# An RWKV block with AdaLN and an FP4 FFN: the last FFNs by chunks in two streams, small weights in one array, FP4 in place

## The chip, the cores and the metric

The kernel runs on one core of a Trainium2 chip. The time is the device time of one execution in microseconds (us). Before the change it is 3216.84 us, the median of three runs (3215.44 to 3220.56). Engine names are those of the profile: PE is the matrix engine (PEld its weight loads), DVE the vector engine, ACT the scalar engine, POOL is GpSimd, SP the engine that issues the DMAs (SPq its queue).

## The reference

The input x is 2 batches of 4096 tokens of 256 channels. Six rows per batch (sa, ca, ga, sb, cb, gb) come from a conditioning vector c: mod = (silu(c) @ wmod).

```python
h = _layernorm(x) * (1 + ca) + sa
x = x + ga * rwkv(h)              # two layers, then a layer norm
h = _layernorm(x) * (1 + cb) + sb
x = x + gb * ffn(h)

# each rwkv layer:
x = x + time_mix(ln(x))           # mixes with the token before, r, k, v, g, decay w, a linear
                                  # recurrence over 4096 tokens, 4 heads of 64
x = x + channel_mix(ln(x))        # sigmoid(. @ cWr) * (relu(. @ cWk)**2 @ cWv), 256 -> 768 -> 256

def ffn(x):                       # 256 -> 704 -> 256
    gate, y = fp4_linear(x, w_gate), fp4_linear(x, w_up)
    return fp4_linear(silu(gate) * y, w_down)
```

fp4_linear rounds both of its operands in blocks of 16 along the last dimension: the block is divided by its largest magnitude over 6, rounded to the grid 0, 0.5, 1, 1.5, 2, 3, 4, 6, and multiplied back. So each FFN rounds its input (256 columns), its hidden row (704 columns) and, once, its weights.

## The kernel before, in words

All arithmetic is in float32. A batch is cut into 16 tiles of 256 tokens (TT), two chunks of 128 (C = 2) each, 32 tiles in all. A tile passes through first_layer, second_layer and ffns, each a Python generator; there are two streams of the first layer (one per batch), two of the second, one for all FFNs, one for the FFN weights and one for the conditioning rows.

The instructions are not issued as the generators yield them. A Plan (lines 104 to 318) records each operation with its costs and its dependences (record, need), and run (from line 280) takes from up to 24 recorded operations of each stream the one that it thinks can start first, by its own table of durations. A stream only records more while the stock of free tiles has at least its number of the tuple LEAST (8, 5, 3). All instructions are given out by line 262, so nearly every row of the profile has that line, and the names of the tiles tell them apart. What the planner chooses is fixed when the program is built: on the chip each engine takes its queue in that order and waits on semaphores.

Tiles: 36 slots of 514 columns, 4 double slots, 24 tiny tiles for row statistics, 5 long tiles of 768 columns for the FFN, 5 PSUM banks (bank), pa and kv for the recurrence.

- The loads (lines 484 to 558): cT in two DMAs, per layer 14 vectors of 256 numbers (vec), w1 in four pieces, w2a, w2b in two, five matrices, td1 and td2 in four pieces, cWk, cWv, cWr, and the modulation weights. The vectors are spread over the partitions number by number. All are issued by SP.
- fp4 (lines 566 to 601): seven DVE operations and one on ACT: largest magnitude, scale, reciprocal, a product into y, the step bits into p, two additions of a large multiple of the step, ACT's subtraction of MAGIC, a product into the destination. It uses the source, y and p; all calls share one tile scales.
- conditioning (from line 1107): the row of ln_out_w lies in one partition of the slot lnw, and POOL's partition_broadcast (line 1118) copies it to all 128 in another slot.
- ffn_weights (from line 1147): after ten steps of the first layer it loads w_gate, w_up and w_down by 128 rows, rounds them, and transposes them on PE.
- ffns (from line 1245), one stream: per tile, layer norm, FP4 of both chunks at once (512 columns), transposes; then, chunk after chunk, gate and up (wg, wu: four groups of 352 columns), FP4 of 704 columns, six transposes, the down product wd, and a multiplication by gb into half of the slot ob. After both chunks POOL adds x over 512 columns and SP stores the tile.

Nothing in ffns records chunk 1 before chunk 0's operations are recorded, and a tile begins after the one before.

Of the kernel before, what the change touches and what calls it, by code (L numbers as in the profile page):

```python
# [37 lines left out]
TINY = 24  # L38
# [3 lines left out]
FFN_SHARE = 1.4  # L42
# [3 lines left out]
MAGIC = 1.5 * 2.0**22  # L46

# [7 lines left out]
    "L0_ffn_w_up", "L0_ffn_w_down", "L0_c", "L0_wmod",  # L55
]
# [47 lines left out]
class Plan:  # L104
# [174 lines left out]

    def run(self, streams, stock):  # L280
        streams = [Stream(*q) for q in streams]
        while True:
# [24 lines left out]
            if not can:  # L307
                assert all(st.gen is None and not st.queue for st in streams), "stuck"
                return
# [72 lines left out]
def rwkv_adaln_fp4_kernel(ctx: ExitStack, tc: tile.TileContext, a: dict, out: bass.AP):  # L382
# [74 lines left out]
    scales = wk.tile([P, 3 * (FI // QB)], F32, name="scales")  # L457

    def take_slot():
        return pl.take(stock)  # L460
# [4 lines left out]
    def give(*ts):  # L465
        stock.extend(ts)
# [23 lines left out]
    with nc.allow_non_contiguous_dma(reason="two vectors of 256"):  # L490
        for b in range(B):
            load(cT[:, :, b], a["L0_c"][b].rearrange("(k p) -> p k", p=P))
# [12 lines left out]
    load(lnw[:1, :D], a["L0_attn_ln_out_w"].unsqueeze(0))  # L505

    def load_mat(name, src, kc):
# [5 lines left out]
    VECS = ["ln1_w", "ln2_w", "x_maa", "w_maa", "k_maa", "v_maa", "r_maa", "g_maa",  # L513
            "gn_w", "gn_b", "ck_maa", "cr_maa", "time_decay", "time_first"]
    lay = []
    for i in range(L):
        w = {}
        vec = const.tile([P, len(VECS), J], F32, name=f"vec{i}")
        for n, v in enumerate(VECS):
            src = a["L0_attn_" + v][i]  # L520
            if v.startswith("time"):
                src = src.rearrange("h k -> (h k)")
            with nc.allow_non_contiguous_dma(reason="a vector of 256"):
                load(vec[:, n, :], src.rearrange("(j p) -> p j", p=P))
            w[v] = vec[:, n, :]

        w1 = a["L0_attn_tm_w1"][i].rearrange("(k p) n -> p k n", p=P)
        w["w1"] = wp.tile([P, J, 8 * E], F32, name=f"w1_{i}")  # L530
        load(w["w1"][:, :, : 5 * E], w1)
        for m in range(5, 8):
            load(w["w1"][:, :, m * E : (m + 1) * E], w1[:, :, 4 * E :])
        w2 = a["L0_attn_tm_w2"][i].rearrange("f e d -> (f e) d")
        w2a = wp.tile([P, D], F32, name=f"w2a_{i}")
        load(w2a, w2[0:P, :])
        w2b = wp.tile([2 * E, D], F32, name=f"w2b_{i}")
        for m in range(2):
            load(w2b[m * E : (m + 1) * E, :], w2[P : 5 * E, :])
        w["w2"] = [w2a[E * f : E * (f + 1), :] for f in range(4)]  # L540
        w["w2b"] = w2b
        for n in ("Wr", "Wk", "Wv", "Wg", "Wo"):
            w[n] = load_mat(f"{n}_{i}", a["L0_attn_" + n][i], J)
        w["wvm"] = const.tile([P, J * H], F32, name=f"wvm{i}")
        w["centred"] = False
        w["td1"] = wp.tile([P, J, 2 * ED], F32, name=f"td1_{i}")
        w["td2"] = wp.tile([2 * ED, D], F32, name=f"td2_{i}")
        for m in range(2):
            load(
                w["td1"][:, :, m * ED : (m + 1) * ED],  # L550
                a["L0_attn_td_w1"][i].rearrange("(k p) n -> p k n", p=P),
            )
            load(w["td2"][m * ED : (m + 1) * ED, :], a["L0_attn_td_w2"][i])
        w["cWk"] = load_mat(f"cWk_{i}", a["L0_attn_cWk"][i], J)
        w["cWv"] = load_mat(f"cWv_{i}", a["L0_attn_cWv"][i], FD // P)
        w["cWr"] = load_mat(f"cWr_{i}", a["L0_attn_cWr"][i], J)
        lay.append(w)
        load_wmod(1 + i)
# [7 lines left out]
    def fp4(nc, src, n, rows, dst, st, y, p):  # L566
# [10 lines left out]

        def blk(t):
            return t[:rows, :n].rearrange("p (b q) -> p b q", q=QB)

        am, sc, inv = (st[:rows, m * (FI // QB) : m * (FI // QB) + nb] for m in range(3))
        sb = src.rearrange("p (b q) -> p b q", q=QB)
        nc.vector.tensor_reduce(am, sb, AX.X, ALU.max, apply_absolute_value=True)
# [4 lines left out]
        nc.vector.scalar_tensor_tensor(blk(y), sb, DOWN, invb, ALU.mult, ALU.mult)  # L588
        nc.vector.tensor_scalar(
            p[:rows, :n].bitcast(I32), y[:rows, :n].bitcast(I32), STEP_BITS, None, ALU.bitwise_and  # L590
        )
        yield
        yv, pv = y[:rows, :n], p[:rows, :n]
        nc.vector.scalar_tensor_tensor(yv, pv, MAGIC, yv, ALU.mult, ALU.add)
        nc.vector.scalar_tensor_tensor(yv, pv, -MAGIC, yv, ALU.mult, ALU.add)
        nc.scalar.activation(yv, yv, AF.Copy, bias=MAGIC)
        yield
        nc.vector.scalar_tensor_tensor(
            dst.rearrange("p (b q) -> p b q", q=QB), blk(y), MAGIC, scb, ALU.subtract, ALU.mult
        )  # L600
# [506 lines left out]
    def conditioning():  # L1107
# [5 lines left out]
        lnb_s, wide_s, tmp_s = take_slot(), take_slot(), take_slot()  # L1113
        lnb = lnb_s[:, :D]
# [3 lines left out]
        pl.gpsimd.partition_broadcast(lnb, lnw[:1, :D])  # L1118
# [25 lines left out]
        give(lnb_s, wide_s, tmp_s, lnw)  # L1144
        tiny.append(few)

    def ffn_weights():
# [3 lines left out]
        for src, dst in ((a["L0_ffn_w_gate"], wg), (a["L0_ffn_w_up"], wu)):  # L1151
            for n0 in range(0, FI, P):
                n = min(P, FI - n0)
                wt, y, p = (pl.take(long) for _ in range(3))
                pl.sync.dma_start(out=wt[:n, :D], in_=src[n0 : n0 + n, :])
                yield from fp4(pl, wt[:n, :D], D, n, wt[:n, :D], scales, y, p)
# [9 lines left out]
                long.extend((wt, y, p))  # L1166
                yield
        for m in range(J):
            wt, y, p = (pl.take(long) for _ in range(3))
            pl.sync.dma_start(out=wt[:, :FI], in_=a["L0_ffn_w_down"][m * P : (m + 1) * P, :])  # L1170
            yield from fp4(pl, wt[:, :FI], FI, P, wt[:, :FI], scales, y, p)
# [10 lines left out]
            long.extend((wt, y, p))  # L1182
# [62 lines left out]
    def ffns():  # L1245
        HF = FI // 2
        while "ffn" not in known:
            yield
        for _ in range(B * NT):
            while not done:  # L1250
                yield
# [5 lines left out]
            xf = xn.rearrange("p c d -> p (c d)")  # L1257
            y_s, p_s = pl.take(long), pl.take(long)
            yield from fp4(pl, xf, C * D, P, xf, scales, y_s, p_s)
            long.extend((y_s, p_s))  # L1260
# [5 lines left out]
            give(xn_s)  # L1266
            yield
            ob_s = take_slot()
            ob = v3(ob_s)
            for c in range(C):  # L1270
                cs_ = slice(c * P, (c + 1) * P)
                hb_s = pl.take(long)
                hb = hb_s[:, :FI]
                for s in range(2):
                    fs = slice(s * HF, (s + 1) * HF)
                    bk, gp = pl.bank()
                    for k in range(J):
                        mm(gp[:, :HF], xqT[:, k, cs_], wg[:, k, fs], k == 0, k == J - 1)
                    pl.scalar.activation(hb[:, fs], gp[:, :HF], AF.Sigmoid)
                    pl.vector.tensor_tensor(hb[:, fs], hb[:, fs], gp[:, :HF], ALU.mult)  # L1280
                    pl.close(bk)
                    yield
                    bk, up = pl.bank()
                    for k in range(J):
                        mm(up[:, :HF], xqT[:, k, cs_], wu[:, k, fs], k == 0, k == J - 1)
                    pl.vector.tensor_tensor(hb[:, fs], hb[:, fs], up[:, :HF], ALU.mult)
                    pl.close(bk)
                    yield
                y_s, p_s = pl.take(long), pl.take(long)
                yield from fp4(pl, hb, FI, P, hb, scales, y_s, p_s)  # L1290
                long.extend((y_s, p_s))
                hT_s = pl.take(long)
                hT = hT_s.rearrange("p (f n) -> p f n", f=NF)
                for g in range(2):
                    bk, pt = pl.bank()
                    for f in range(3):
                        at0 = f_at[3 * g + f]
                        tr(pt[:, f * P : (f + 1) * P], hb[:, at0 : at0 + P])
                    pl.scalar.copy(
                        hT[:, 3 * g : 3 * g + 3, :], pt[:, : 3 * P].rearrange("p (f n) -> p f n", f=3)  # L1300
                    )
                    pl.close(bk)
                    yield
                long.append(hb_s)
                bk, y = pl.bank()
                for f in range(NF):
                    mm(y[:, :D], hT[:, f, :], wd[:, f, :], f == 0, f == NF - 1)
                pl.vector.tensor_tensor(ob[:, c, :], y[:, :D], rows["gb"][b], ALU.mult)
                pl.close(bk)
                long.append(hT_s)  # L1310
                yield
            give(xq_s)
            pl.gpsimd.tensor_tensor(ob, ob, x1, ALU.add)
            pl.sync.dma_start(out=rows_of(out, b, t), in_=ob)
            give(ob_s, x1_s)
            yield

# [4 lines left out]
    with tc.manual_schedule():  # L1322
        streams += [(ffns(), LATE[2], LEAST[2]), (ffn_weights(), 2.0, 0), (conditioning(), -1.0, 0)]
        pl.run(streams, stock)

# [20 lines left out]
```

## Time and profile before

| | |
|---|---|
| median of three runs | 3216.84 us |
| the profiled execution | 3216.25 us |
| its span, first to last instruction | 3214.5 us |
| mean granted PE clock | 0.970 |
| PE busy | 3034.9 us, 94% |
| DVE busy | 2386.1 us, 74% |
| ACT, POOL busy | 1621.0 us, 937.6 us |
| moved by DMA | 42.31 MB, 13 GB/s mean |

The profile divides the span into 40 slices and gives each engine a digit, its busy share in tenths. The table of stages gives busy microseconds of each engine in a chosen stretch, with the number of instructions in brackets, then the granted clock of PE (1.00 is full speed), the mean busy share of the 16 DMA engines and what they moved in GB/s. In the timeline a line begins with the start and the duration in us; in square brackets stands how long the engine had been idle, and who released it. A line of the waits gives the total in us, how often, and the longest. Transposes are matmuls with ident. A float32 matmul shows as two instructions.

### The profile page before, as it was taken

To read this page: it belongs to the slowest core of one execution; us is meant where nothing else is said; L and a number is where in the kernel's file an instruction comes from. 1 tells how busy PE (TensorE), PEld (TensorE's weight loads), DVE (VectorE), ACT (ScalarE), POOL (GpSimd) and SP (SyncE) were. 2 spreads that over 40 slices of the span, in tenths; PEclk is the share of its full clock that TensorE was granted. 3 is DMA by queue.
4 is the path that set the end of the run, shared out by engine and by line. 5 is a ranking of instruction groups with operands and counts; after the bars stand their busy time and mean duration, and the time that the engine had idled before them with its cause. 6 is when DMAs were issued, how large, how long until landed. Compare 5 with 4: busy or idle time off the path is not lost.

```text
span 3214.5 us, 88104 instructions
## 1 busy us (share of the span) xinstructions
PE 3034.9 (94%) x37948; PEld 2423.3 (75%) x37948; DVE 2386.1 (74%) x6146; ACT 1621.0 (50%) x3244; POOL 937.6 (29%) x857
## 2 busy tenths in 40 slices
PE   3899999999999999999999999999999999999875
PEld 2677778787777778788777777878787787778653
DVE  4687777787877777777777876787787787777764
ACT  1465554555555555555555454555554555554321
POOL 1233332232323333223223232233233233322210
PEclk7899999999999999999999999999999999999987
DMA  4000000000000000000000000000000000000000
GB/s 130 17 20 5 9 8 8 12 15 8 9 8 8 15 9 15 8 6 11 8 15 8 8 11 5 18 5 14 8 9 8 12 11 9 11 2 14 12 4 10
DMA packets 46856, 42.31 MB, mean 13 GB/s; under 512 B 13185, under 2 KB 44930, under 8 KB 46466
## 3 DMA queue, kind: packets, MB, share of 16 engines
q1 hardware_dynamic: 46466, 36.68, 3.8%
q8 instruction: 298, 4.88, 0.6%
q14 instruction: 92, 0.75, 0.1%
HBM read 28.28 MB, written 8.39 MB: 11 GB/s over the span
## 4 chain that ended last, share of the span: by engine, by line
PE 77%; DVE 10%; ACT 6%; issue 3%; POOL 1%; DMA 1%; SPq 1%; POOLq 0%; DVEq 0%; ACTq 0%
PE bank L262 69%; PE pa L262 7%; DVE slot L262 5%; ACT slot L262 3%; DVE long L262 2%; ACT attn L262 2%; DVE tiny L262 1%; PE kv L262 1%; DVE scales L262 1%; POOL slot L262 1%; SPq L485 1%; DVE diag L262 1%; ACT L262 1%; ACT long L262 1%; POOL tiny L262 0%
## 5 line engine op out<-in xcount | busy, mean ns | idle before, releaser
L262 POOL TENSOR_TENSOR slot<-slot,slot 128x512 f32<-128x512 f32 x416 | 503.5, 1224 | 980.0 <-DVE slot L262 692.5
L262 ACT ACTIVATE slot<-bank 128x512 f32<-128x512 f32 (+1 forms) x644 | 338.2, 530 | 692.7 <-PE bank L262 662.1
L262 POOL TENSOR_TENSOR tiny<-tiny,nhalf 128x2 f32<-128x2 f32 (+1 forms) x288 | 291.6, 1015 | 957.5 <-DVE tiny L262 867.3
L262 DVE TENSOR_TENSOR slot<-slot,slot 128x512 f32<-128x512 f32 x512 | 382.7, 749 | 102.4 <-PE pa L262 86.3
L262 PE MATMUL bank<-slot,cWk 128*128 128x256 f32 x1536 | 367.4, 385 | 2.8 <-DVE slot L262 1.7
L262 PE MATMUL bank<-cWv,slot 128*128 128x256 f32 x1536 | 344.1, 380 | 0.0
L262 PEld LDWEIGHTS pa<-slot 64*32 64x32 f32 x19456 | 222.1, 108 | 140.3 <-issue 54.6
L262 PEld LDWEIGHTS bank<-slot,cWk 128*128 128x128 f32 x1536 | 286.4, 191 | 45.7 <-DVE slot L262 2.8
L262 PEld LDWEIGHTS bank<-cWv,slot 128*128 128x128 f32 x1536 | 289.3, 190 | 39.6 <-ACT slot L262 0.3
L262 ACT ACTIVATE slot<-bank,vec 128x256 f32<-128x256 f32 x512 | 233.1, 496 | 154.2 <-PE bank L262 145.7
L262 DVE TENSOR_TENSOR slot<-slot,bank 128x512 f32<-128x512 f32 x192 | 131.0, 682 | 225.8 <-PE bank L262 203.6
L262 PE MATMUL pa<-slot 64*32 64x16 f32 x19456 | 264.2, 190 | 30.4 <-DVE slot L262 10.6
L262 DVE SCALAR_TENSOR_TENSOR slot<-bank,vec,slot 128x256 f32<-128x256 f32 x640 | 273.7, 473 | 18.8 <-PE bank L262 18.2
L262 POOL TENSOR_TENSOR slot<-slot 128x512 f32<-128x512 f32 x128 | 142.1, 1112 | 329.2 <-ACT slot L262 278.4
L262 DVE TENSOR_TENSOR long<-long,bank 128x352 f32<-128x352 f32 x256 | 131.8, 515 | 91.3 <-ACT long L262 67.6
L262 PE MATMUL bank<-ident,slot 128*128 128x128 f32 x1152 | 177.6, 282 | 23.1 <-ACT slot L262 15.9
L262 ACT ACTIVATE slot<-slot,tiny 128x256 f32<-128x256 f32 x256 | 142.1, 594 | 111.8 <-DVE tiny L262 90.3
L262 PE MATMUL bank<-wd,long 128*128 128x256 f32 x768 | 191.6, 402 | 0.2 <-ACT slot L262 0.2
L262 DVE SCALAR_TENSOR_TENSOR slot<-slot,vec,slot 128x256 f32<-128x256 f32 x384 | 179.3, 503 | 12.6 <-POOL slot L262 12.5
L262 ACT ACT_TABLE_LOAD x137 | 175.8, 1283 | 19.2 <-PE bank L262 9.5
L262 ACT COPY slot<-bank 128x512 f32<-128x512 f32 x224 | 130.0, 583 | 103.5 <-PE bank L262 99.5
L262 PE MATMUL bank<-wg,slot 128*128 128x352 f32 x512 | 177.8, 470 | 4.1 <-ACT slot L262 4.1
(112 smaller groups left out, 5796.3 us busy)
## 6 DMA issues: line engine op xcount, KB each, us to landing
slot<-in_L_attn_x_dram SPq DMA_DIRECT2D x64, 256.0 KB, 2.7
out_dram<-slot SPq DMA_DIRECT2D x32, 256.0 KB, 2.2
slot<-in_L_wmod_dram SPq DMA_DIRECT2D x6, 256.0 KB, 6.7
cWk<-in_L_attn_cWk_dram SPq DMA_DIRECT2D x2, 768.0 KB, 5.9
cWv<-in_L_attn_cWv_dram SPq DMA_DIRECT2D x2, 768.0 KB, 6.6
long<-in_L_ffn_w_down_dram SPq DMA_DIRECT2D x2, 352.0 KB, 2.8
long<-in_L_ffn_w_gate_dram SPq DMA_DIRECT2D x5, 128.0 KB, 4.9
long<-in_L_ffn_w_up_dram SPq DMA_DIRECT2D x5, 128.0 KB, 2.0
```

The source lines that it names most:

```text
L262: fn(*[real(v) for v in a], **{n: real(v) for n, v in k.items()})
L485: nc.sync.dma_start(out=dst, in_=src)
```

## The change

1. The loads. Two arrays are made from the inputs ahead of the launch: small, 1564 columns for each layer, which holds the 14 vectors, w1, td1, w2a, w2b and td2 in the form in which the kernel uses them, and cT. One DMA loads each layer's array. The names w["w1"] and so on become views of it.
2. The row ln_out_w is loaded into all 128 partitions by one DMA with a broadcast source; partition_broadcast is gone, and so is its slot.
3. fp4 works in the tile that holds its source (y is the source); it takes one further tile p. There are three tiles scales, one for inputs and weights, and one per chunk.
4. ffns becomes ffn_inputs, ffn_chunk and ffn_chunks. For all but the last three tiles ffn_inputs runs the chunks itself, one after the other. For the last three (FFN_TAIL) it puts them into the list ready[c], and two further streams, one per chunk number, take them from there; the next tile's input is begun when both lists are shorter than FFN_AHEAD.
5. Each chunk has its own output slot, an add on POOL of 256 columns and a store of 128 rows.
6. 16 tiny tiles in place of 24. When no recorded operation can start, a new function press lets one stream record more, whatever the stock.

```diff
-TINY = 24
+TINY = 16
+FFN_TAIL = 3
+FFN_AHEAD = 1
...
+    def press(self, streams):
+        for st in sorted(streams, key=lambda st: st.least):
...
             if not can:
+                if self.press(streams):
+                    continue
...
-    load(lnw[:1, :D], a["L0_attn_ln_out_w"].unsqueeze(0))
+    load(lnw[:, :D], a["L0_attn_ln_out_w"].unsqueeze(0).to_broadcast([P, D]))
...
-        vec = const.tile([P, len(VECS), J], F32, name=f"vec{i}")
+        small = wp.tile([P, SMALL], F32, name=f"small{i}")
+        load(small, a["small"][i])
...
-    def fp4(nc, src, n, rows, dst, st, y, p):
+    def fp4(nc, t, n, rows, st, p):
...
+        y, pv = t[:rows, :n], p[:rows, :n]
+        yb = y.rearrange("p (b q) -> p b q", q=QB)
...
+        nc.vector.scalar_tensor_tensor(yb, yb, DOWN, invb, ALU.mult, ALU.mult)
+        nc.vector.tensor_scalar(pv.bitcast(I32), y.bitcast(I32), STEP_BITS, None, ALU.bitwise_and)
+        yield
+        nc.vector.scalar_tensor_tensor(y, pv, MAGIC, y, ALU.mult, ALU.add)
+        nc.vector.scalar_tensor_tensor(y, pv, -MAGIC, y, ALU.mult, ALU.add)
+        nc.scalar.activation(y, y, AF.Copy, bias=MAGIC)
+        yield
+        nc.vector.scalar_tensor_tensor(yb, yb, MAGIC, scb, ALU.subtract, ALU.mult)
...
-        pl.gpsimd.partition_broadcast(lnb, lnw[:1, :D])
...
+    def ffn_inputs():
...
+        for n in range(B * NT):
+            while not done or max(len(q) for q in ready) >= FFN_AHEAD:
                 yield
...
+            for c in range(C):
+                if n < B * NT - FFN_TAIL:
+                    yield from ffn_chunk(c, b, t, x1_s, xq_s, left)
+                else:
+                    ready[c].append((b, t, x1_s, xq_s, left))
...
+    def ffn_chunks(c):
+        for _ in range(FFN_TAIL):
+            while not ready[c]:
                 yield
+            yield from ffn_chunk(c, *ready[c].pop(0))
...
+        pl.gpsimd.tensor_tensor(ob, ob, x1[:, c, :], ALU.add)
+        pl.sync.dma_start(out=rows_of(out, b, t)[:, c, :], in_=ob)
...
+        streams += [(ffn_inputs(), LATE[2], LEAST[2]), *((ffn_chunks(c), LATE[2], 1) for c in range(C)), (ffn_weights(), 2.0, 0), (conditioning(), -1.0, 0)]
```

ffn_chunk is the body of the loop over c of ffns, with scales[1 + c], a p tile of its own, and the slot ob_s taken at the scaling.

## The prediction

> **What bounds it now.** I read the page first: engine shares, then the 40 slices.
>
> ```profile
> PE 3034.9 (94%) x37948; PEld 2423.3 (75%) x37948; DVE 2386.1 (74%) x6146; ACT 1621.0 (50%) x3244; POOL 937.6 (29%) x857
> ...
> PE   3899999999999999999999999999999999999875
> ...
> PEclk7899999999999999999999999999999999999987
> ```
>
> PE is busy in 94% of the span, and the missing part lies in the first and the last slices. The table of stages gives it in us (columns: PE, weight loads, DVE, ACT, POOL, clock, DMA).
>
> ```profile
> 300.00:2950.00 2650.00, 2609.01 (x33224) 2095.83 (x33223) 2028.14 (x5218) 1416.52 (x2824) 816.72 (x728) 0.99 0.03 10
> ```
> ```profile
> 3147.00:3165.40 18.40, 9.97 (x34) 7.03 (x34) 10.72 (x23) 2.67 (x5) 0.87 (x1) 0.78 0.00 0
> 3165.40:3185.00 19.60, 11.65 (x38) 8.13 (x38) 11.80 (x21) 3.89 (x7) 1.26 (x1) 0.76 0.04 13
> ...
> sum 117.60, PE 63.11 PEld 44.15 DVE 63.13 ACT 17.53 POOL 6.40; mean PE 9.02 PEld 6.31 DVE 9.02 ACT 2.50 POOL 0.91
> ```
>
> In the middle PE idles 41 of 2650 us: it is the bound, and only less PE work would help there. In the last 117.6 us (from 3096.9, when the last channel mix leaves PE) PE and DVE are each busy 63 us, taking turns. The waits of PE after 2950 name the turn:
>
> ```profile
> PE bank L262 <- DVE long L262: 48.3, 6, 9.4
> ```
>
> Six times PE waits for one FP4 rounding on DVE, with nothing else to do: five times 7.3 to 8.5 us, once 9.4. The start, from the timeline (PE, POOL, SP, DVE):
>
> ```profile
> 14.36 6.62 PE L262 MATMUL bank<-slot,slot 128*128 128x512 f32 x8 [14.36 <-DMA slot<-in_L_wmod_dram]
> 36.51 1.39 PE L262 MATMUL bank<-ident,slot 128*128 128x128 f32 x4 [15.54 <-ACT slot L262]
> 56.34 0.69 PE L262 MATMUL bank<-ident,long 128*128 128x128 f32 x2 [18.43 <-DVE long L262]
> ```
> ```profile
> 25.23 0.55 POOL L262 PARTITION_BROADCAST slot<-slot  x1 [6.29 <-issue]
> 34.90 0.73 POOL L262 TENSOR_TENSOR tiny<-tiny,nhalf 128x2 f32<-128x2 f32 x1 [9.12 <-issue]
> ```
> ```profile
> 45.35 16.92 SPq L262 DMA_DIRECT2D long<-in_L_ffn_w_gate_dram  x4
> ```
> ```profile
> 52.61 0.42 DVE L262 TENSOR_REDUCE scales<-long 128x16 f32<-128x256 f32 x1 [16.79 <-DMA long<-in_L_ffn_w_gate_dram]
> ```
>
> PE stops at 21 and works steadily only from 56.34. The first stop is POOL's: around one partition_broadcast of 0.55 us it does nothing else from 18.94 to 34.90, and the layer norm's power stands behind it. The second is the first w_gate tile: its load is issued last, at 45.35, lands at 52.6, and DVE rounds it until 56.34 (3.73 us). PE takes its queue in order, so the first projection waits behind that tile's transposes.
>
> **Start: small weights in one array, row spread by its load.** Ahead of w_gate, SP now issues 77 loads of vectors, matrices, modulation weights and x, about 0.5 us each, until 45. In the order of the changed program it issues 28 loads ahead: 14 us by the same step. What remains is bytes: the layer arrays hold 0.80 MB each, the matrices and the rest bring it to 10.25 MB including the first w_gate tile, nearly what moves today. Between 16 and 26 us the DMA queue moved 309 GB/s at 97% busy, and its best slices 381; from 2.8 us (issue at 0.7, first landing 2.1 later) the tile lands at 29.7 (381) to 36.0 (309). I take 33, between the two, as many of the packets that slowed the 309 stretch (704 of 3077 under 512 B) are gone. With 3.73 of rounding PE resumes at 36.7 instead of 56.34: **minus 20** (16.6 to 23). The other chain, layer norm of the first x, has its power input at 23.2 today and needs 5.9 more (34.90 to the end of the lerp in today's steps), or 29 to 31; it is the next in line, so 26 is the most.
>
> Against it: layer 0's array and seven matrices now stand ahead of the modulation weights, 4.21 MB to their end: 13.9 to 16.4 us where PE starts at 14.36 today. That costs at most 2, before the w_gate wait, and is hidden by it. The broadcast's removal alone is worth nothing: PE would wait for w_gate. The row's own load grows from 1 to 128 KB, 0.4 us of the queue at 309 GB/s, counted in the bytes. The page "DMA: Bandwidth & Descriptors", section "Anatomy of one DMA", of the Trainium skill prices transfers at 2.0 us plus bytes at 436 GB/s; by that estimate the tile would land near 26 and the layer norm's chain would decide, 26 us saved in place of 20; no stretch here holds that rate.
>
> **Tail: the last three FFNs by chunks in two streams.** Row prices, DVE: FP4 of 704 columns 0.88+0.20+0.42+0.94+0.54+1.86+0.94=5.78, with ACT's 0.79 and gaps 6.65 (3178.38 to 3185.03); FP4 of 512: 4.46, with ACT 5.1; a gating product 0.52. PE: a gate or up group 1.18 (3191.59 to 3192.78), six transposes 1.5, twelve down matmuls 4.4 to 5.3 after a wait. I call T0 the end of the last channel mix on PE, and walk the changed order from there:
> - DVE does the channel mix's end and most of the last tile's two layer norms, 6 us, until tile 31's first gate is there at T0+8 (PE first has six and four transposes and one down product). Then in its order: 8 products (4.2), two FP4 (11.6), two scalings (0.8), and of the last tile the norm's rest (2.5) and FP4 (4.5): 23.6, to T0+31. The last tile's own input is ready at about T0+26.
> - PE: two groups of it, then transposes of tile 31's second chunk at T0+31 (1.5), a group (1.2), a down product (4.2), two groups (2.4): T0+40.5.
> - Last tile, chunk 0: its FP4 with chunk 1's products between is 10.3, to T0+51; transposes and down to 56.7; chunk 1's FP4 has ended at 55 beside that; transposes 1.5, down 4.4: 62.6; scaling 0.4, POOL add 1.0, store 3.05 (3211.45 to the end): **T0+67**, against 117.6 now.
> - T0 itself is later: five groups, six transposes and a down product now stand before it: 5.9+1.5+2.8 (the down product takes 2.76 at 1517 us, full clock) = 10. PE idled 12.5 in 2950 to 3096.9, which may hide part; I count none as hidden.
> Gain 117.6-67-10: **minus 40**. Low end 20: if each of the three tiles still exposes one FP4 (3x6.65). High end 50: if the 12.5 idle us take the moved work.
>
> The clock enters here: in the tail's rows it is 0.76 to 0.78, and 0.99 in the middle; the down product takes 4.74 at 3166.93 and 2.76 at full clock. The page "TensorE: Matmul & The Clock Gate", section "HAM oscillation", says that the clock halves after an idle gap over some 3.4 us; by that rule the 10 us gap before the last chunk would still make the end cold, so the end would not speed up; were the gaps shorter than that, four down products would save some 1.7 us each, 7 in all, by that estimate. My walk keeps the slow price after each wait.
>
> **Middle: FP4 in place, chunked adds and stores.** FP4 has the same seven DVE operations and one ACT; only the tile that holds the result changes, and a chunk holds two long tiles, not three. Both programs have the same 19,760 matmuls of the same shapes. One 128x512 POOL add (1.22) becomes two of 128x256, which the trace does not show: between 0.82 (128x2) and 1.22 each, so 0.4 to 1.2 more a tile, 13 to 39 over 32 tiles; POOL is 29% busy, and while POOL's other adds stand behind these, PE, 98% busy there, has other streams' work. 32 more stores at about 0.4 of SP's time hide in a DMA share of 0.03. Tables: 129 loads, not 137 (1.28 each), on ACT at 50%. Tiny tiles 24 to 16 and three scale tiles: no wait on them above 1.4 us now. The planner's order is new throughout, so PE's 41 us of waits may move either way: 0, with plus or minus 15 (a third of them).
>
> **Sum.** 3214.5-20-40 = 3154.5. The profiled execution took 3216.25, 1.75 more than its span, and lies 0.6 under the median of 3216.84: **3157**.
>
> **Rivals.**
> - One end only, **3177**: either the start keeps its wait (bytes at under 200 GB/s would do it, as the 124 GB/s of 26 to 37 us show can happen when SP issues slowly), or DVE, with 22.5 us a tile against PE's 21.6 (the two rows above, added), becomes the tail's bound and each tile exposes an FP4. For: DVE and PE are level in the tail. Against: one FP4 beside the other chunk's groups is what the changed order has on both engines.
> - No measurable change (within 0.2%, 6.4 us, about what this measurement can tell): the middle loses the 60.
> - Slower, **3253**: PE's order in the middle is fixed at build time, and a chunk's transposes stand in it where the planner thinks FP4 done. If they stand too early, PE waits in each of 29 tiles for three FP4s (input and two chunks). The waits of PE on DVE's long tiles between 300 and 2950 are three, 1.5 us in all, the longest 1.1: 87 x 1.1 = 96 on 3157. It decides from 0.76 us a wait. For: FFN work is placed anew. Against: the same rounding, the same planner, and 1.5 us of such waits now.
>
> **Numbers.** Forecast 0.68 (3133 to 3172: start 16.6 to 26, tail 31 to 50, middle as above), one end only 0.20 (3172 to 3195), no change 0.04, slower 0.08. Faster 0.88. The range 3130 to 3190 leaves out the last two and a part of the second.
>
> **What would show it.** Start: PE's first transposes of w_gate at 33 to 40 us, no gap on POOL before the second power, SP's w_gate issue near 15. Tail: PE's waits on long after the last channel mix from 48 to under 20 us, the span from there 67 and not 117.6, PE and DVE busy side by side. Middle: 41 us idle of 2650, give or take 15. I am wrong if PE resumes after 45, if the FFN streams wait for each other's tiles, or if PE's idle time between 300 and 2950 rises above 60.

## The result, and the profile after

The changed kernel takes **3185.45 us** (median of four runs, 3183.25 to 3188.18), the kernel before 3216.41 beside it (3215.44 to 3220.56): ratio 0.9902, 95% interval 0.9885 to 0.9919. That is 28 us over the predicted 3157 and inside the range of 3130 to 3190, but outside the forecast's own band of 3133 to 3172. The profiled execution took 3185.40 us, its span is 3183.6.

The page of the kernel after, engine shares and two rows of the slices:

```profile
PE 3034.4 (95%) x37948; PEld 2428.1 (76%) x37948; DVE 2390.7 (75%) x6146; ACT 1616.2 (51%) x3236; POOL 951.1 (30%) x888
...
PE   5899999999999999999999999998999999999987
...
PEclk8899999999999999999999999999999999999989
```

PE is busy for as long as before (3034.9), so the 31 us that the span lost are idle time of PE. The first digit went from 3 to 5, the last two from 7 and 5 to 8 and 7. Between them a single 8 is new, in the slice from 2149 to 2229 us; a wait of 7.3 us in it belongs to the hole that the experiments come back to. The start in the timeline of after (PE, then DVE, POOL, SP):

```profile
14.34 5.11 PE L271 MATMUL bank<-slot,slot 128*128 128x512 f32 x8 [14.34 <-DMA slot<-in_L_wmod_dram]
23.64 0.33 PE L271 MATMUL bank<-ident,slot 128*128 128x128 f32 x1 [4.19 <-ACT slot L271]
...
35.96 0.69 PE L271 MATMUL bank<-ident,long 128*128 128x128 f32 x2 [10.93 <-DVE long L271]
```
```profile
32.23 0.42 DVE L271 TENSOR_REDUCE scales<-long 128x16 f32<-128x256 f32 x1 [9.28 <-DMA long<-in_L_ffn_w_gate_dram]
```
```profile
22.05 0.70 POOL L271 TENSOR_TENSOR tiny<-tiny,nhalf 128x2 f32<-128x2 f32 x1 [4.33 <-DVE tiny L271]
```
```profile
24.72 14.55 SPq L271 DMA_DIRECT2D long<-in_L_ffn_w_gate_dram  x5
```

The first matmul stands where it stood; the w_gate tile lands at 32.2 and no longer at 52.6, and PE goes on at 35.96 and not at 56.34. POOL's power (of the layer norm) is at 22.05, not at 34.90. Stages of after (columns as before: PE, weight loads, DVE, ACT, POOL, clock, DMA):

```profile
300.00:2950.00 2650.00, 2582.99 (x33007) 2072.34 (x33006) 2004.55 (x5137) 1386.82 (x2770) 814.00 (x741) 0.99 0.03 10
...
3125.25:3145.00 19.75, 13.22 (x54) 9.13 (x52) 18.87 (x45) 4.51 (x9) 2.47 (x3) 0.97 0.02 7
3145.00:3165.00 20.00, 19.25 (x72) 14.41 (x72) 12.07 (x23) 5.05 (x10) 2.03 (x2) 0.86 0.04 13
3165.00:3183.60 18.60, 9.19 (x36) 7.20 (x36) 9.24 (x15) 3.40 (x6) 1.45 (x2) 0.82 0.05 16
```

The middle idles 67 us where it idled 41. The tail, from the end of the last channel mix, is 58.3 us where it was 117.6, and in its middle third PE is busy 19.25 of 20 us. The waits of PE after 2950, which were 48.3 us in six:

```profile
PE bank L271 <- DVE long L271: 12.9, 3, 6.8
```

To compare whole programs I divide each span in three: start (0 until PE works steadily: its first w_gate transposes, in the last row of the table the first projection), middle (from there to the end of the last channel mix on PE) and tail. Idle is the stretch less PE's busy time in the table of stages. The last four columns add up to the span. They come from one profiled execution each, and executions of one program differ: 25 of before, beside start_only, took 3200.68 to 3225.93 us, the shortest at a granted clock of 0.975 and the longest at 0.968. So differences of some 10 us in the last column may lie in the execution as well as in the program. b_soon41's profiled execution is its shortest, 3247.51 against a median of 3260.04, so its columns add up to less than its ratio says.

| kernel | ratio to before | start | middle | tail | PE busy |
|---|---|---|---|---|---|
| before | 1 | 48.4 | 76.8 | 54.5 | 3034.9 |
| after | 0.9902 | 29.6 | 102.9 | 16.7 | 3034.4 |
| start_only | 0.9983 | 28.7 | 92.4 | 46.4 | 3036.9 |
| tail_only | 0.9999 | 50.9 | 96.5 | 28.8 | 3038.5 |
| tail0 | 1.0014 | 29.5 | 99.8 | 46.7 | 3035.8 |
| b_row | 0.9982 | 49.9 | 78.8 | 54.4 | 3026.5 |
| b_soon41 | 1.0161 | 49.6 | 114.7 | 46.4 | 3034.6 |
| b_ahead23 | 0.9902 | 50.1 | 80.8 | 39.0 | 3018.6 |
| cap2 | 0.9847 | 28.9 | 90.3 | 19.0 | 3024.7 |
| a_soon45 | 0.9868 | 27.9 | 96.4 | 20.0 | 3025.5 |
| cap2_soon45 | 0.9870 | 29.6 | 100.4 | 20.6 | 3028.3 |
| mkfix | 0.9914 | 30.8 | 101.7 | 16.9 | 3030.7 |
| best1 | 0.9889 | 30.3 | 96.7 | 17.5 | 3027.0 |
| mk_thr20 | 0.9822 | 11.6 | 93.3 | 28.8 | 3027.2 |

Before to after: -18.8, +26.1, -37.8 and -0.5 of busy time, -31.0 in all, as the spans say. The start and the tail came as forecast, in idle time. **The middle gave back 26 us.** The theory: every edit makes the planner write another fixed order, and the middle's waits come with that order; one hole in it is caused by finished tiles that wait for the FFN. Rivals: the streams themselves, or the new loads, cost the middle those 26 us; or the order of before is typical of its code and it is the new code that costs.

### The profile page after: what moved, and what is told of

It reads as the page before. It is cut to its first block, busy times and chain, and to the rows that moved or that the text cites. A ratio compares the mean times of both kernels' runs of the same rounds, so it can differ in the third digit from the quotient of the medians.

```text
span 3183.6 us, 88202 instructions
## 1 busy us (share of the span) xinstructions
PE 3034.4 (95%) x37948; PEld 2428.1 (76%) x37948; DVE 2390.7 (75%) x6146; ACT 1616.2 (51%) x3236; POOL 951.1 (30%) x888
## 4 chain that ended last, share of the span: by engine, by line
PE 77%; DVE 12%; ACT 6%; issue 3%; POOL 2%; DMA 1%; SPq 0%; POOLq 0%; ACTq 0%; DVEq 0%
PE bank L271 69%; PE pa L271 7%; DVE slot L271 5%; ACT slot L271 4%; DVE long L271 3%; ACT attn L271 2%; DVE tiny L271 1%; PE kv L271 1%; DVE scales L271 1%; POOL slot L271 1%; POOL tiny L271 1%; DVE diag L271 1%; ACT long L271 0%; DMA small<-in_small_dram 0%; DMA long<-in_L_ffn_w_gate_dram 0%
## 5 line engine op out<-in xcount | busy, mean ns | idle before, releaser
L271 POOL TENSOR_TENSOR slot<-slot,slot 128x512 f32<-128x512 f32 (+1 forms) x448 | 516.6, 1166 | 1034.0 <-DVE slot L271 652.9
L271 PE MATMUL bank<-slot,small 32*128 32x256 f32 (+2 forms) x2304 | 433.9, 408 | 4.4 <-ACT slot L271 3.6
L271 PEld LDWEIGHTS bank<-slot,small 32*128 32x128 f32 (+2 forms) x2304 | 276.3, 189 | 87.0 <-issue 31.2
L271 DVE SCALAR_TENSOR_TENSOR slot<-bank,small,slot 128x256 f32<-128x256 f32 x640 | 273.5, 472 | 26.9 <-PE bank L271 26.4
L271 ACT ACTIVATE slot<-bank,small 128x256 f32<-128x256 f32 x512 | 234.2, 497 | 99.8 <-PE bank L271 96.9
L271 ACT ACTIVATE slot<-slot 128x512 f32<-128x512 f32 x288 | 180.9, 631 | 35.3 <-DVE slot L271 30.4
L271 DVE SCALAR_TENSOR_TENSOR slot<-slot,small,slot 128x256 f32<-128x256 f32 x384 | 180.9, 503 | 10.5 <-POOL slot L271 10.4
```

Of the source, the lines that this page charges most:

```text
L271: fn(*[real(v) for v in a], **{n: real(v) for n, v in k.items()})
```

## The experiments

All times are compared with the kernel before, run beside it on the same chip.

**One half at a time.** start_only is the kernel before with the new loads and the row by its load:

```diff
+        small = wp.tile([P, SMALL], F32, name=f"small{i}")
+        load(small, a["small"][i])
-        pl.gpsimd.partition_broadcast(lnb, lnw[:1, :D])
```

> The kernel before with the change's loads alone (one array of small weights per layer, cT in one load, ln_out_w spread by its load); FFNs and FP4 as before. Theory (three separate terms: start -20, tail -38, middle +26, the last from streams that run out of free slots): PE resumes at about 36 us, the tail stays near 117 us, so 3196, give or take 15 for the new order of the middle. Rival (the start is worth nothing, because work then waits elsewhere in the filling of the streams): within 5 of 3216. Rival (the middle's loss belongs to the loads' new order): above 3205 with 25 us more idle PE in the middle.

3205.44 against 3213.25, ratio 0.9983 (0.9967 to 0.9998). In the table the start gains all of its 19.7, and the middle takes back 15.6 though no line of the FFN is changed. The tail didn't stay near 117 us as expected: it is 96.0 us long and idles 46.4, 8.1 less than before, with the FFN code of before. tail_only is the reverse, the kernel after with the 77 loads and the broadcast of before:

```diff
-        load(small, a["small"][i])
+        pl.gpsimd.partition_broadcast(lnb, lnw[:1, :D])
```

> The changed kernel with the loads of before (77 of them, partition_broadcast). Theory: start as before (PE resumes at 56), tail near 58 us, middle loses some 20: 3205, give or take 15. Rival (the middle's loss comes from the loads' order, not from the FFN's restructuring): near 3178, with PE's idle time in the middle as before, about 77 us.

3213.62, ratio 0.9999 (0.9985 to 1.0012): the tail gains 25.7 of idle time, the middle loses 19.7 and the start 2.5. The tail near 58 us was missed: it is 100.3 us long, as 71.5 us of PE's work stand in it where after has 41.7. Each half alone loses 16 to 20 in the middle, both together 26: the losses don't add, which speaks against a fixed price of either part. tail0 undoes the two streams alone:

```diff
-FFN_TAIL = 3
+FFN_TAIL = 0
```

> The changed kernel with FFN_TAIL = 0: all FFNs by one stream; up to the tail PE's order is the same as in the changed kernel. Theory: the two streams are worth all of the tail's gain, 54.5 - 16.7 = 38 us of idle PE: 3223, slower than before the change, and the middle idles 100 us as in the changed kernel. Rival (part of the tail's gain comes from in-place FP4 and chunked stores): at or under 3210.

3219.7, ratio 1.0014 (0.9997 to 1.0031), 1.1% above the kernel after. The middle is as in after (99.8), so the streams don't cost it; the tail is back to six waits, in the waits of PE after 2950 of tail0:

```profile
PE bank L271 <- DVE long L271: 41.5, 6, 9.8
```

This is the worth of the streams with nearly the same order ahead of them: 30.0 us of idle time. I expected 38; the other 7.8 of the tail's 37.8 are not theirs, and start_only gained as much (8.1) with the FFN code of before.

**The row alone** (b_row): the kernel before, edited only where lnw is loaded and used.

```diff
-    load(lnw[:1, :D], a["L0_attn_ln_out_w"].unsqueeze(0))
+    load(lnw[:, :D], a["L0_attn_ln_out_w"].unsqueeze(0).to_broadcast([P, D]))
-        pl.gpsimd.partition_broadcast(lnb, lnw[:1, :D])
```

> The kernel before with one edit: the row ln_out_w is spread over the partitions by its load, partition_broadcast is gone; the 77 loads stay. My claim was that this is worth nothing alone, because PE waits for the first w_gate tile. Expected: POOL's gap of 9 to 16 us around the broadcast gone, its second power at 20 to 25 us instead of 34.9, PE's first transposes of w_gate at 56 to 58 as before, and the time within 3 us of the kernel before. Rival (POOL's gap is part of PE's wait): PE resumes 5 us earlier or more, and the time falls by as much.

3211.36 against 3216.49, ratio 0.9982 (0.9968 to 0.9996), a little more than the 3 us I allowed. PE and POOL in its timeline:

```profile
24.31 0.33 PE L262 MATMUL bank<-ident,slot 128*128 128x128 f32 x1 [3.93 <-ACT slot L262]
...
56.59 0.69 PE L262 MATMUL bank<-ident,long 128*128 128x128 f32 x2 [31.25 <-DVE long L262]
```
```profile
22.72 0.70 POOL L262 TENSOR_TENSOR tiny<-tiny,nhalf 128x2 f32<-128x2 f32 x1 [4.10 <-DVE tiny L262]
```

POOL is 12.2 us earlier and PE's first transposes too (24.31, 36.51 before), and then PE waits 31 us for w_gate in place of 18 and resumes at 56.59. At the start the broadcast's removal is worth nothing, as argued; the 5 us stand in PE's busy time, 8.4 less. The clock goes with it: by the clock records of the two traces PE works 125.0 us at half clock in before and 106.6 in b_row. If half of that time is what the half clock costs, that is 9.2 us, an estimate.

**The hole.** At 2137 to 2162 us of after nearly all work belongs to one FFN tile (two operations of a layer end on ACT until 2139.8). The timeline of PE and, in the second fence, of POOL:

```profile
2140.24 1.07 PE L271 MATMUL bank<-ident,slot 128*128 128x128 f32 x4 [2.68 <-DVE slot L271]
2142.03 2.71 PE L271 MATMUL bank<-wg,slot 128*128 128x352 f32 x4 [0.72 <-ACT slot L271]
...
2148.21 1.35 PE L271 MATMUL bank<-wu,slot 128*128 128x352 f32 x4
2156.86 1.54 PE L271 MATMUL bank<-ident,long 128*128 128x128 f32 x6 [7.31 <-DVE long L271]
2158.33 4.06 PE L271 MATMUL bank<-wd,long 128*128 128x256 f32 x12
```
```profile
2162.94 0.84 POOL L271 TENSOR_TENSOR slot<-slot,slot 128x256 f32<-128x256 f32 x1 [26.65 <-DVE slot L271]
```

Only FFN tiles appear on PE: nothing of the four layer streams is queued between. My explanation is the stock: too few slots are free here for a layer stream to record (LEAST asks for 8 and 5), because finished tiles that wait for the FFN hold the others. The stock stands in no trace, so only the experiment speaks for it. cap2 lets no second-layer tile begin while two finished ones wait:

```diff
-            while not between[b]:
+            while not between[b] or len(done) >= 2:
```

> The changed kernel in which a second layer begins no tile while two finished tiles wait for their FFN (one condition more in second_layer). Theory (between 2137 and 2162 us all layer streams stood still because finished tiles held the slots): that hole is gone, with it some 12 to 20 us: 3165 to 3173. Rival (the finer adds and stores and in-place FP4 cost the middle a little in each tile): no change, 3180 to 3190. Rival (luck of the order alone): the hole goes, another comes, 3170 to 3200.

3162.7, ratio 0.9847 (0.9827 to 0.9868). The same stretch in the tables of stages of after and of cap2:

```profile
2137.00:2162.00 25.00, 14.30 (x41) 9.39 (x42) 10.05 (x16) 7.68 (x12) 0.00 (x0) 0.73 0.02 6
```
```profile
2137.00:2162.00 25.00, 24.78 (x124) 19.31 (x122) 12.68 (x31) 8.28 (x17) 8.89 (x9) 1.00 0.00 1
```

The hole is gone, and the middle idles 90.3 in place of 102.9, 12.6 less, with the rest of the gain in PE's busy time (-9.7). The stretch itself idles 10.7 us in after and 0.2 in cap2. So the hole is some 11 to 13 of the 26, as far as cap2, which is another order too, can tell. It isn't needed for a loss, though: in start_only and tail_only the middle loses 16 to 20 and no stretch of 25 us between 300 and 2950 holds more than 5 us of idle time.

**Other orders of the same work.** SOON and AHEAD_OPS (the 24 recorded operations of each stream) are constants of the planner. They change no operation of the kernel, only the order (and with it how often ACT loads a table).

```diff
-SOON = 40.0
+SOON = 41.0
```

> The kernel before with SOON = 41.0 in place of 40.0, a number of the planner by which it takes an older operation first if that could start at most so many ns later; the work and the loads are the same. Theory (the middle's idle time depends on where the planner's order happens to run streams dry, as much as on the change): moves by 5 to 30 us from 3216, most likely slower, with start (56) and tail (near 117) unmoved. Rival (the middle's idle time belongs to the kernel's work and is the same for any such order): within 5 us of 3216.

On the kernel before: 3260.04 against 3210.61, ratio 1.0161 (1.0144 to 1.0179), more than the 5 to 30 us I expected; the middle idles 114.7. PE resumes at 56.97 as expected, but the tail moved, to 96.2 us. With 45.0 on the kernel after:

> The changed kernel with SOON = 45.0. Theory of order: the middle's idle time moves by 5 to 25 us, here most likely down: 3165 to 3182; PE resumes at 36 as before. Rival (steady cost of finer grains in the middle): 3183 to 3190.

3168.28, ratio 0.9868 (0.9854 to 0.9883); the middle idles 96.4. Both together, cap2 and 45.0:

> The kernel after with two edits, each of which gained alone: no second-layer tile is begun while two finished tiles wait for the FFN (3162.7), and SOON 45 (3168.3). If these two take away separate losses, their gains add: 3185-22-17, 3143 to 3150. If each edit only draws a new fixed order, with PE's idle time between its resumption and the last channel mix anywhere from 90 to 115, then they do not add: 3158 to 3185, worse than the cap alone as likely as better.

3177.56, ratio 0.9870 (0.9850 to 0.9890), no better than the cap alone (the intervals overlap) and far from the 3143 to 3150 of gains that add: two edits that each gain don't add. Last, the kernel before with

```diff
-AHEAD_OPS = 24
+AHEAD_OPS = 23
```

> The kernel before with AHEAD_OPS 23 instead of 24: the same instructions, another fixed order. If the kernel before has an order that is favourable by chance (PE idles 77 us between its resumption and the last channel mix, where eight other orders have 90 to 115), this one has 85 to 115 there and the time is 5 to 40 us longer, less what the tail gains or loses. Rival (the order of before is typical of its code, and it is the new code that costs): 70 to 85 there, time 3200 to 3225.

3186.04, ratio 0.9902 (0.9887 to 0.9917): **one number gains as much as the whole change.** My expectation for the middle (85 to 115) failed; it is 80.8, as the rival had it, though its time (3200 to 3225) is missed too. The gain is in the tail, 86.4 us long with four waits, and in PE's busy time (-16.3). The waits of PE after 2950 and the tail in the table of stages of b_ahead23:

```profile
PE bank L262 <- DVE long L262: 30.4, 4, 8.5
```
```profile
3102.10:3188.50 86.40, 47.43 (x163) 33.19 (x160) 46.42 (x86) 13.97 (x26) 5.76 (x5) 0.80 0.03 9
```

So the 117.6 us that the change was measured against were partly an order's, not the code's. The spread of the middle is 77 to 115 in five programs with the FFN code of before, and 90 to 103 in the nine with the new.

**The start further.** mkfix lets the modulation weights and x load first (a scratch tile of the masks held their place) and leaves the order of the arithmetic:

```diff
-TINY = 16
+TINY = 13
-    with tc.tile_pool(name="mk", bufs=1) as mk:
+    if True:
+        mk = const
```

> The changed kernel with the five scratch tiles of the masks in memory of their own (TINY 13 pays for them), so that the modulation weights and x need not wait for the masks and go out first; each compute engine's order stays as in the changed kernel. Theory: PE's first matmul at 10 in place of 14.3, but PE still waits for the first w_gate tile, which lands at 32 as before: 3185 within 3. Rival (the layer norm's chain decides the start): 4 to 5 us faster.

3182.98 against 3210.61, ratio 0.9914 (0.9899 to 0.9929). PE in its timeline:

```profile
4.45 5.37 PE L271 MATMUL bank<-slot,slot 128*128 128x512 f32 x8 [4.45 <-DVE slot L271]
...
37.37 0.69 PE L271 MATMUL bank<-ident,long 128*128 128x128 f32 x2 [21.56 <-DVE long L271]
```

Ten us earlier at the first matmul, nothing at the end: w_gate's wait takes it all. mk_thr20 is mkfix with that wait out of the way as well, the FFN weights after 20 steps and not 10:

```diff
-        while steps[0, 0] < 10:
+        while steps[0, 0] < 20:
```

> The kernel after with two edits at the start: the mask scratch tiles don't block the first loads (wmod and x land first), and the FFN weights are loaded, rounded and transposed after 20 steps of the first layer instead of 10. If PE's wait at 20 to 36 us is the first w_gate tile alone, PE starts on the first layer as soon as layer norm of x and the layer's matrices are there: steady work from 20 to 26 us, the idle time of the start falls from 30 to under 22, the middle is a new order and may cost as much again (planned middle idle a little lower than after). Time 3165 to 3185. Rival (the layer's own matrices are as late as w_gate): PE still resumes at 33 to 37 and the start gains nothing.

PE in its timeline, after the first matmul at 4.45:

```profile
15.07 1.40 PE L271 MATMUL bank<-ident,slot 128*128 128x128 f32 x4 [4.54 <-ACT slot L271]
19.03 3.78 PE L271 MATMUL bank<-slot,small 128*128 128x256 f32 x8 [2.57 <-DVE slot L271]
```

**3160.87 against 3216.49, ratio 0.9822 (0.9805 to 0.9838)**, the fastest here, though not apart from cap2's interval. PE works from 19.03; the start idles 11.6 instead of 29.6. The rival (the layer's matrices are as late) is out. The new order gives 12 back in the tail (28.8).

best1, cap2 with mkfix's edit and FFN_TAIL 4, shows once more that gains don't add:

> The changed kernel with the cap of two waiting tiles, FFN_TAIL = 4 and the mask tiles in memory of their own. Theory: the cap's gain and a tail some 5 us shorter: 3160 to 3170. Rival: no better than the cap alone.

3172.65, ratio 0.9889 (0.9862 to 0.9915). Its tail is the shortest (47.1 us), and 18.7 us of idle time stand between 2950 and the last channel mix, 12.3 in cap2.

## Why the prediction was right, and where it was wrong

**Start, right.** The w_gate tile was put at 33 and landed at 32.2; PE at 36.7, was 35.96; the first matmul at 13.9 to 16.4, was 14.34; the layer norm of x at 29 to 31, was 27.0 (POOL's addition at 25.99 and 1.04). The claim that bytes decide when the tile lands held. In the table of stages of after, from the first landing to the tile:

```profile
2.80:32.20 29.40, 6.34 (x12) 2.68 (x12) 9.96 (x38) 3.42 (x6) 3.60 (x6) 0.86 1.00 355
```

The DMA engines are full (1.00) at 355 GB/s, within the 309 to 381 of the working. A sub-step was wrong without effect: SP issues w_gate at 24.72, not near 15; its 28 loads take 0.86 us each on average, not 0.5. The page "DMA: Bandwidth & Descriptors" of the Trainium skill, section "Anatomy of one DMA", would by its 436 GB/s, a fit for DMAs that GpSimd issues, land the tile near 26, an estimate; these loads are SP's, and the measured 355 decides. That PE's wait is this tile alone is shown by mk_thr20, where it goes on at 19.03.

**Tail, right in sum by two errors.** The last channel mix's end to the end of the span was put at 67 us and is 58.3; the work moved ahead of it at 10, and PE's busy time in the tail fell by 21.4 (63.1 to 41.7). In idle time the forecast of 40 stands beside 37.8. Waits on long went from 48 to 12.9, under the 20 that I set. In the tail of after, two FP4s in a row on DVE expose one:

```profile
3145.27 1.54 PE L271 MATMUL bank<-ident,long 128*128 128x128 f32 x6 [6.79 <-DVE long L271]
...
3147.46 4.35 PE L271 MATMUL bank<-wd,long 128*128 128x256 f32 x12
...
3155.85 2.75 PE L271 MATMUL bank<-wd,long 128*128 128x256 f32 x12
```

The down product after the wait is slow (4.35), the next is at full clock (2.75): I kept the slow price for all.

**Middle, wrong.** The step that failed is "so PE's 41 us of waits may move either way: 0, with plus or minus 15 (a third of them)". Measured: 41.0 to 67.0 between 300 and 2950, over the 60 at which I called myself wrong, and +26.1 from PE's resumption to the last channel mix. The parts that I priced came as priced: POOL's add of 128x256 takes 0.84 and POOL's busy time rose by 13.5 (13 to 39), ACT's table loads fell from 137 to 129. What was mis-sized is the spread of an order. A third of the waits was a guess, and nothing in the working says what an order can cost; b_soon41, which changes nothing else, moves the middle by 38.

Of the 26, some 11 to 13 are the hole (cap2). The rest is spread over many short waits, as the waits of PE in after between 300 and 2950 show (before: 7.6 in 16, 4.7 in 9, 1.5 in 3):

```profile
PE bank L271 <- ACT slot L271: 9.3, 16, 1.9
PE pa L271 <- DVE slot L271: 8.9, 15, 1.4
PE bank L271 <- DVE long L271: 8.4, 4, 7.3
```

The 7.3 is the hole's; b_ahead23, with the FFN code of before, has one as long for an FP4 too, at 1959 (7.30). The other waits **stay open**: whether the new code's orders are worse on average or merely drawn (90 to 103 against 77 to 115) these programs don't settle. PE's busy time, too, differs by up to 20 us between orders of the same 37,948 instructions; where it differs most, most of that goes with the clock. By the clock records of the traces PE works 125.0 us at half clock in before, 99.8 in b_ahead23, 132.9 in after and 118.0 in cap2; half of each difference, an estimate of its cost, is 12.6 of b_ahead23's 16.3 and 7.5 of cap2's 9.7. The rest isn't assigned.

**The rivals.** "One end only" (3177, 3172 to 3195, with 0.20) has the measured time in its band but isn't what happened: both ends gained. So the number is right only because the stated range took in part of that rival's band; of the 60 us forecast 31 came. As the size of the middle was a guess, that it took no more was luck. "Slower" priced transposes placed too early in every tile; at that length it happened in one, at 2156.86, where PE waits 7.31. "No change: the middle loses the 60" was the right place at less than half the size, with 0.04.

## What to carry to other kernels

Where a planner fixes the order at build time, an edit is measured together with a new order: first take the spread from some programs that differ in the order alone (here -1.0% and +1.6% from one constant each), and judge edits by the idle time of their own stage. A wait is worth its removal only when the next one behind it is known: 10 us earlier at the first matmul gave nothing, and 18 us once the tile behind it had moved too. Look for stretches where one chain has every engine; here a cap on finished work, one line, removed one.

## What the runs showed of the hardware

The clock falls after shorter pauses than I had thought. In the hole of after (table of stages):

```profile
2137.50:2140.20 2.70, 0.07 (x2) 0.00 (x0) 1.90 (x3) 2.35 (x5) 0.00 (x0) 1.00 0.04 9
2140.20:2142.00 1.80, 1.07 (x4) 0.67 (x4) 0.00 (x0) 0.88 (x3) 0.00 (x0) 0.53 0.00 0
2142.00:2144.50 2.50, 2.47 (x4) 1.51 (x5) 0.00 (x0) 1.28 (x1) 0.00 (x0) 0.50 0.00 0
...
2147.00:2149.50 2.50, 2.50 (x9) 1.36 (x7) 1.04 (x2) 0.47 (x1) 0.00 (x0) 0.97 0.00 0
```

After an idle time of 2.68 us PE runs at half clock, until about 2147. Earlier in after, where PE had been busy throughout from 1110 to 1117.6, still less was enough (timeline of PE, then the table of stages):

```profile
1119.04 0.73 PE L271 MATMUL pa<-slot 64*32 64x16 f32 x64 [1.39 <-DVE slot L271]
```
```profile
1119.10:1119.70 0.60, 0.60 (x64) 0.57 (x64) 0.60 (x5) 0.47 (x1) 0.00 (x0) 1.00 0.03 14
1119.80:1126.50 6.70, 6.70 (x114) 4.66 (x114) 4.62 (x13) 0.21 (x1) 2.14 (x2) 0.50 0.02 5
```

One wait of 1.39 us stands ahead of 6.7 us at half clock, so a short wait can cost more than its own length. Not every such wait does this: after one of 2.51 us that ends at 2045.85 the clock stays at 1.00. These runs don't show what decides. The page "TensorE: Matmul & The Clock Gate", section "HAM oscillation", warns of gaps over some 3.4 us; here 2.68 was enough once, and 1.39 once. In the tail of after the waits of 6.79 and 5.88 agree with it (the down products behind them take 4.35 and 4.15, others 2.75 to 2.86).

A partition_broadcast that the profile shows with 0.55 us cost POOL 12 us: without it, in b_row, the power behind it starts at 22.72 and not at 34.90.
